# Graph network in two passes: degrees and relation counts turned in 32x32 blocks on VectorE and spread by DRAM reloads, instead of by TensorE

## The chip, the cores and the metric

The kernel runs on one core of one Trainium2 chip. The metric is the device time of one execution in microseconds (us), as the median over runs. The profile is of one execution on the same core, recorded by the hardware profiler.

## What is computed

The input `x` is (128 graphs, 64 nodes, 768 features), `adj` a 0/1 matrix (128, 64, 64), the same for both layers. In layer 0 `adj` also serves as the relation index, and the reference is written for general relation numbers.

```
# layer 0
h   = relu(layernorm(x))
deg = adj.sum(-1);  rdeg = adj^T.sum(-1);  deg_c, rdeg_c = (the same, 1 where 0)
ctx = adj   @ (h @ Wadj.T + badj) / deg_c
    + adj^T @ (h @ Wrev.T + brev) / rdeg_c
    + h @ Wself.T + bself
rel = einsum(adj,   E[rels]) @ Wr.T  + br  * deg
    + einsum(adj^T, E[rr])   @ Wrr.T + brr * rdeg      # rr: reversed relations, NUM_BASE higher
x   = x + ctx + rel
# layer 1
h    = relu(layernorm(x))
hw   = h @ W (6 heads of 128);  logits from tanh(hw), w_src, w_dst;  leaky relu; masked by adj
out  = softmax(logits) @ hw + b;  elu;  gate = sigmoid(h @ H_w.T + H_b)
x    = x + gate * out + (1 - gate) * h
```

## The kernel before

**Tiling.** A tile is 128 rows of 768 features, two graphs (GT = 2, N = 64). Two tiles make a pair; there are NT = 64 tiles and NP = 32 pairs. Pass 1 does layer 0 for pair after pair, pass 2 layer 1. In pass 1 the three operands of a pair (graph average with `adj`, with its transpose, and the rows themselves) meet the three weights. The products over 3x3 blocks of the weights are done as 15 products with sums of blocks (a fast matrix product, `PRODUCTS`, with the operand sums `f1` to `f11` formed on VectorE by `form`, L351 and L353). Pair 0 uses plain products (`PLAIN`).

**Steps and their order.** `main(p)` gives a list of about 91 steps, one per (product, k block, operand): each step is one f32 128x128 by 128x256 matmul (L754), which the profile shows as two records. After the last step of a product that is read out, `add` (L746, L748) adds or subtracts its PSUM bank (`pwa`, `pwb`, or one half of `pwcd`) into `X`. `beside(p)` lists the other work: what finishes pair p - 1 and what prepares pair p + 1. The table `BESIDE` gives the step of `main` ahead of which each piece is issued. `merged` weaves the two lists. All engines and the DMA queue of SyncE (SP) are in program order, so `BESIDE` fixes the order on each queue. Pairs 2 to 31 are in `SHARED`: for them the own rows come as turned blocks by `turn_own`, `put_own` (L551) and `load_own` (L565) through DRAM.

**Degrees.** `degrees` (step "deg") multiplies a block matrix of ones (`blkb`) with the bf16 adjacency on TensorE (L607), so that every row of a graph holds the column sums; VectorE clamps them out of PSUM (L609). `one_over` (step "over") takes the reciprocal over 256 columns (L613), and `over_degrees` (step "rts") multiplies the adjacency by it (L618) into `rts`, which the operand matmuls (`operands`, L682, step "ops") use as moving data; ScalarE copies their results out of PSUM (L692).

**Counts.** `prep_c`, `ids_worth` and `ids_sum` count on VectorE how often each relation number occurs in a row of the adjacency (packed as digits), and `digits` (step "dig") unpacks them to `cnt`, 81 values per row (78 counts, two flags, one 1). GpSimd (POOL) writes each value three times in a row into `c3` (L653). `count_t` (steps "ct0" and "ct1") transposes `c3` on TensorE in two parts per tile, 126 and 117 columns (L661), and ScalarE copies them out to `cntT` (L664). `counts` (L738) multiplies `cntT` with the table `tabs`, in which each of the 81 rows stands as three bf16 parts, and accumulates into the bank of the product that is read next. So `cntT` of pair p + 1 is made ahead of step 90 of pair p and first read after product a01 of pair p + 1 (steps 12 to 17).

PSUM: `pwa` and `pwb` have one bank each, `pwcd` two; the buffer `pb` (two of them) is shared by the degree product, the count transposes and the operand matmuls.

## Time and profile before

| | |
|---|---|
| median of 3 runs | 2358.45 us (2357.53 to 2358.49) |
| profiled execution | 2358.5 us, span 2356.7 us |
| mean granted TensorE clock | 0.994 |
| pass 1 ends (last `pwcd` count matmul) | 1425.4 us |
| degree products L607 on TensorE | 32, mean duration 273 ns |
| count transposes L661 on TensorE | 128, median duration 219 ns |
| copies of the counts L664 on ScalarE | 128, median 269 ns |
| reciprocal L613 on VectorE | 32, mean 1744 ns |
| copies L653 on POOL | 64, mean 436 ns |

In the page's rows a group is given as line, engine, operation, out<-in, shapes, count, then busy us and mean ns, then the idle time of the engine ahead of it with what ended it. PE is TensorE's matmul stream and PEld its weight loads, DVE is VectorE, ACT ScalarE. A timeline row gives the start, the length, and the operation with a count of merged instructions. Matmuls are pipelined: a record's duration overlaps with the next one's.

### The profile page before, as it was taken

Reading aid. Unit: us, or ns where it says so; the run is one execution under the profiler, and the core shown is the slowest. Engines: PE = TensorE matmul, PEld = TensorE weight load, DVE = VectorE, ACT = ScalarE, POOL = GpSimd, SP = SyncE. Lnnn points to the kernel's source line nnn. Section 1 sums busy time; section 2 is a strip of 40 time slices with the busy share of each in tenths; the row PEclk is TensorE's granted clock in tenths of the full one; section 3 lists DMA queues with packets and bytes.
Section 4 is the critical chain, followed back from the end, with each engine's and each line's share of the span. In section 5 each row is a group of like instructions: output and inputs, shape, how many; then the busy total and the mean of one; then the engine's idle time right before and its main releaser. Section 6 shows DMA issues by size and latency. Waiting matters only on the chain.

```text
span 2356.7 us, 35546 instructions
## 1 busy us (share of the span) xinstructions
PE 2326.5 (99%) x11591; PEld 1654.2 (70%) x11591; DVE 1979.0 (84%) x3673; ACT 1304.5 (55%) x3955; POOL 434.1 (18%) x983
## 2 busy tenths in 40 slices
PE   9999999999999999999999999999999999999996
PEld 7888888888888888888888885444444444444444
DVE  8878778777787787787787777899999999999997
ACT  3454454454554554554554533677766776777775
POOL 1111111111111111111111111122222222222222
PEclk9999999999999999999999999999999999999997
DMA  6334435335335335335334357577777776676776
GB/s 188 83 90 125 119 90 136 106 90 143 100 93 147 93 97 152 90 96 147 90 103 139 90 162 145 117 146 142 152 144 150 141 148 140 138 145 138 148 136 132
DMA packets 706907, 296.19 MB, mean 126 GB/s; under 512 B 524586, under 2 KB 657053, under 8 KB 706722
## 3 DMA queue, kind: packets, MB, share of 16 engines
q1 hardware_dynamic: 696850, 269.11, 46.5%
q0 software_dynamic: 9728, 24.78, 6.0%
q8 instruction: 91, 1.49, 0.3%
q14 instruction: 94, 0.77, 0.1%
q10 hardware_dynamic: 144, 0.04, 0.0%
HBM read 131.85 MB, written 136.45 MB: 114 GB/s over the span
## 4 chain that ended last, share of the span: by engine, by line
PE 94%; DVE 2%; DMA 2%; issue 1%; ACT 0%; SPq 0%; POOL 0%; POOLq 0%; DVEq 0%; ACTq 0%
PE pwa L754 21%; PE pwb L754 17%; PE pwcd L754 14%; PE pma L1059 13%; PE pmb L1059 11%; PE pmd L1059 5%; PE pmc L1059 4%; PE pb L682 3%; PE ps L1224 1%; PE pwcd L738 1%; PE pwcd L682 1%; DVE weights L353 1%; PE ps L1163 1%; DMA weights<-in_wrev_t_dram 1%; PE pmc L1224 0%
## 5 line engine op out<-in xcount | busy, mean ns | idle before, releaser
L754 PE MATMUL pwa<-weights,op 128*128 128x256 f32 x2304 | 539.4, 381 | 0.3 <-DVE x L746 0.3
L754 PEld LDWEIGHTS pwa<-weights,op 128*128 128x128 f32 x2304 | 422.3, 190 | 53.8 <-issue 1.1
L754 PE MATMUL pwb<-weights,op 128*128 128x256 f32 x1932 | 454.5, 381 | 0.0
L754 PEld LDWEIGHTS pwb<-weights,op 128*128 128x128 f32 x1932 | 359.4, 190 | 53.1 <-issue 0.2
L353 DVE TENSOR_TENSOR op<-op 128x768 f32<-128x768 f32 x310 | 291.5, 949 | 95.6 <-ACT op L692 91.7
L754 PE MATMUL pwcd<-weights,op 128*128 128x256 f32 x1560 | 357.8, 379 | 0.0
L754 PEld LDWEIGHTS pwcd<-weights,op 128*128 128x128 f32 x1560 | 296.1, 190 | 40.1
L1059 PE MATMUL pma<-weights,op_f 128*128 128x512 f32 x620 | 291.2, 592 | 0.0
L1111 ACT ACTIVATE pr<-pr 128x128 f32<-128x128 f32 x768 | 225.6, 295 | 92.3 <-DVE pr L1101 90.5
L692 ACT COPY op<-pb 128x512 f32<-128x512 f32 (+1 forms) x132 | 70.8, 618 | 320.5 <-PE pb L682 320.5
L1059 PEld LDWEIGHTS pma<-weights,op_f 128*128 128x128 f32 x620 | 117.7, 190 | 147.4 <-issue 139.0
L330 POOL TENSOR_SCALAR rn<-su 128x1 f32<-128x1 f32 x124 | 28.1, 227 | 901.9 <-ACT hf L325 531.0
L1059 PE MATMUL pmb<-weights,op_f 128*128 128x512 f32 x372 | 180.9, 594 | 0.0
L540 ACT ACTIVATE hp<-x,rn 128x768 f32<-128x768 f32 x60 | 107.8, 1797 | 109.7 <-POOL rn L332 109.7
L1111 ACT ACTIVATION_READ_ACCUMULATOR pr<-pr 128x1 f32 x768 | 143.6, 187 | 0.0
L324 ACT ACTIVATE hf<-x 128x768 f32<-128x768 f32 x64 | 53.6, 837 | 150.1 <-DVE x L790 150.1
L1184 ACT ACTIVATE pb<-al,mx 128x64 f32<-128x64 f32 x384 | 128.1, 336 | 12.3 <-DVE mx L1176 12.2
L1059 PEld LDWEIGHTS pmb<-weights,op_f 128*128 128x128 f32 x372 | 68.4, 190 | 84.0 <-issue 75.8
L1285 POOL DMA_DIRECT2D out_dram<-f x62 | 55.0, 887 | 390.0 <-DVE f L1282 382.6
L746 DVE TENSOR_TENSOR x<-pwa,x 128x256 f32<-128x256 f32 x96 | 40.4, 421 | 99.8 <-PE pwa L738 72.0
L1059 PE MATMUL pmb<-weights,h 128*128 128x512 f32 x248 | 122.5, 596 | 0.0
L1059 PE MATMUL pmc<-weights,op_f 128*128 128x512 f32 x248 | 121.8, 592 | 0.0
(232 smaller groups left out, 4219.3 us busy)
## 6 DMA issues: line engine op xcount, KB each, us to landing
x<-in_x_dram SPq DMA_DIRECT2D x64, 384.0 KB
h<-ht SPq DMA_DIRECT2D x64, 384.0 KB
out_dram<-x SPq DMA_DIRECT2D x64, 384.0 KB
hh<-hh SPq DMA_DIRECT2D x64, 384.0 KB
h<-h SPq DMA_DIRECT2D x256, 96.0 KB
x<-hh SPq DMA_DIRECT2D x64, 384.0 KB
out_dram<-f POOLq DMA_DIRECT2D x62, 384.0 KB, 6.5
h<-hpt SPq DMA_DIRECT2D x60, 384.0 KB
```

What stands on the lines that cost most here:

```text
L324: nc.scalar.activation(by, src, AF.Copy, scale=-1.0 / D, accum_out=sums[:, 0:1])
L330: nc.gpsimd.tensor_scalar(to[:, 0:1], sums[:, 1:2], 1.0 / D, EPS, op0=OP.mult, op1=OP.add)
L353: return (nc.vector.tensor_add if s1 == "+" else nc.vector.tensor_sub)(to, x, y)
L540: nc.scalar.activation(hp.rearrange("p (b f i) -> p b f i", b=KB, f=NQ), X[t].rearrange("p (b i f) -> p b f i", b=KB, f=NQ), AF.Relu, scal ...
L682: nc.tensor.matmul(to[:, g, :, i, :], H0[2 * p + k][o, kb * P : (kb + 1) * P], rts[p % 2][o, k, :n].rearrange("p s n -> p (s n)"), start=T ...
L692: nc.scalar.copy(a[:, :n].rearrange("p s h (g n) -> p g (s h) n", g=GT), ps[:, :, c * n * KQ * N : (c + 1) * n * KQ * N].rearrange("p g (x ...
L746: nc.vector.tensor_add(v, bank[b][:, :CQ], v)
L754: nc.tensor.matmul(bank[b][:, :CQ], OPS[p, an][:, s, q, :], bw[bn][:, (s * KQ + q) * CQ : (s * KQ + q + 1) * CQ], start=(first and q == s ...
L1059: nc.tensor.matmul(bank[p, b], operand(p, an)[:, q, :], bw2[bn][:, 2 * q * CQ : 2 * (q + 1) * CQ], start=(first and q == 0), stop=(q == KQ ...
L1111: nc.scalar.activation(PR[t][:, j, h, :], PR[t][:, j, h, :], AF.Copy, accum_out=to)
L1184: nc.scalar.activation(PB[t][:, h, :], AL[t][:, h, :], AF.Exp, bias=MX[t][:, h : h + 1], accum_out=DN[t][:, h : h + 1])
L1285: nc.gpsimd.dma_start(of[t * P : (t + 1) * P, :], FF[t], accum_op=OP.add)
```

## The change

For pairs 2 to 31 the degree product on TensorE is replaced. VectorE reduces the adjacency along the row, for it and its transpose (`row_degrees`; the numbers of the column sums are the row sums of the other one), clamps and inverts the 4 columns, and turns a 128x32 tile in 32x32 blocks; the turned block goes to DRAM (`put_degrees`) and comes back with each graph's degrees spread over its 64 partitions (`get_degrees`). `over_row_degrees` then multiplies as before.

The counts of these pairs are placed by POOL in six copies into one standing tile `c3s` of 2 tiles x 2 parts x 128 columns, turned by one VectorE instruction of 512 columns (`turn_counts`), stored to DRAM (`put_counts`), and read back so that the blocks come to their places (`get_counts`). The table is laid out anew: two parts of 128 rows each, the unused rows zero. Pairs 0 and 1 keep the degree product and the transposes on TensorE, with `c3s` written by ScalarE and one copy out of PSUM per tile. The diff, with lines left out of the table `BESIDE`:

```diff
--- before.py
+++ after.py
@@ -83,14 +83,7 @@
 IN_PLACE = {"f3": "a12", "f2": "a10"}
-BESIDE = {... "f2": 20, "f3": 21, "dev1": 22, "deg": 26, "prepc": 26, ... "over": 36, ... "rts": 48, ...
-          "dig": 67, "a01": 68, "load": 68, "eturn1": 79, "etput1": 82, "ops": 83, "f1": 83, "f7": 83,
-          "ct0": 88, "ct1": 89}
+BESIDE = {... 'f2': 20, 'deg': 20, 'f3': 21, 'dev1': 22, 'putd': 24, 'prepc': 26, ... 'getd': 34, ...
+          'rts': 50, ... 'dig': 67, 'a01': 68, 'load': 68, 'ct': 75, 'putct': 78, 'eturn1': 79,
+          'etput1': 82, 'ops': 83, 'f1': 83, 'f7': 83, 'getct': 87}
 PLACES = ("g6", "g10", "b11", "b21", "g12", "w", "g14", "b01", "b10", "b20", "b02", "b12", "b22",
@@ -225,10 +218,9 @@
     NROW = NCNT + 3
-    PARTS = ((0, P // 3), (P // 3, NROW))
     assert NV == 3 * NG and DIGIT ** 3 <= 1 << 24
     assert GT == 2 and N == 64 and DO == P and H == KB and KB % 6 == 0 and H % 2 == 0
-    assert 3 * (NROW - P // 3) <= P and NT % 2 == 0 and HALF <= 512
+    assert 2 * 32 <= NROW and 3 * NROW <= 2 * P and NT % 2 == 0 and HALF <= 512
     xf = x.rearrange("g n d -> (g n) d")
     of = out.rearrange("g n d -> (g n) d")
@@ -244,6 +236,8 @@
     H0D = [dram.tile([KB * P, P], F32, name=f"h0_{t}") for t in range(NT)]
+    CTD = [dram.tile([4 * P, P], BF16, name=f"ct_{p}") for p in range(NP)]
+    RDD = [dram.tile([Q, P], F32, name=f"rd_{p}") for p in range(NP)]
     PTD = [dram.tile([KB // 2 * P, P], F32, name=f"pt_{t}") for t in range(NT)]
     H1D = [[dram.tile([KB * P, P], F32, name=f"h1_{p}_{k}") for k in range(2)] for p in range(NP)]
@@ -461,7 +455,18 @@
         nc.vector.tensor_copy(identb, ident)
-        tabs = [wa.tile([3 * (b - a), D], BF16, name=f"tab{a}") for a, b in PARTS]
+        tabs = wa.tile([P, 2, D], BF16, name="tabs")
+        R2 = NROW - 2 * Q
+        PLACED = ((0, 0, 0, 0, Q), (1, 1, 0, 0, Q), (2, 2, 0, 0, Q), (0, 3, 0, Q, Q), (1, 4, 0, Q, Q),
+                  (2, 5, 0, Q, Q), (0, 6, 0, 2 * Q, R2), (1, 7, 0, 2 * Q, R2),
+                  (2, 6, R2, 2 * Q, Q - R2), (2, 7, R2, 3 * Q - R2, 2 * R2 - Q))
+        nc.vector.memset(tabs[:, 1], 0.0)
+        c3s = wa.tile([P, 2, 2, P], BF16, name="c3")
+        nc.vector.memset(c3s, 0.0)
+        dgs = wa.tile([P, Q], F32, name="dgs")
+        nc.vector.memset(dgs, 0.0)
@@ -521,8 +526,10 @@
             nc.scalar.copy(q[:NROW], v[:NROW])
             if i < 2:
                 nc.vector.tensor_sub(v[:NROW], v[:NROW], q[:NROW])
-            for (a, b), tab in zip(PARTS, tabs):
-                nc.sync.dma_start(tab[i : 3 * (b - a) : 3, :], q[a:b, :])
+            for c, f, at, v0, n in PLACED:
+                if c == i:
+                    a = NQ * at + f % NQ
+                    nc.sync.dma_start(tabs[a : a + NQ * (n - 1) + 1 : NQ, f // NQ, :], q[v0 : v0 + n, :])
         H0, ADF, AB, CNT, CT_T, GR, WO, SUM, HF, HH_, HT = ({} for _ in range(11))
         OPS = {}
@@ -578,13 +585,47 @@
                 nc.vector.tensor_copy(af, AI[p])
                 nc.vector.tensor_copy(ab, af)
+        DGR, RD = {}, {}
+        def row_degrees(p):
+            dg = DGR[p] = small.tile([P, 2, 2], F32, name="dg")
+            nc.vector.tensor_reduce(dg, ADF[p], AX.X, OP.add)
+        def turn_degrees(p):
+            row_degrees(p)
+            d = dgs
+            v = d[:, :4].rearrange("p (k d) -> p k d", k=2)
+            nc.vector.tensor_scalar(v, DGR[p], 1.0, None, op0=OP.max)
+            nc.vector.reciprocal(v, v)
+            RD[p] = small.tile([P, Q], F32, name="dt", bufs=1)
+            nc.vector.transpose(RD[p], d)
+        def put_degrees(p):
+            nc.sync.dma_start(RDD[p].rearrange("c (b n) -> b c n", n=Q), RD[p])
+        def get_degrees(p):
+            rd = RD[p] = work.tile([P, 4, N], F32, name="rd", bufs=1)
+            for g in range(GT):
+                at = RDD[p][0:4, g * N : (g + 1) * N]
+                nc.sync.dma_start(rd[g * N : (g + 1) * N],
+                                  bass.AP(tensor=at.tensor, offset=at.offset,
+                                          ap=[[0, N], *at.ap]))
+        def over_row_degrees(p):
+            rd = RD[p].rearrange("p (k d) n -> p k d n", k=2)
+            for d in range(2):
+                nc.vector.tensor_mul(rts[p % 2][:, :, d, :], ADF[p][:, :, 1 - d, :], rd[:, :, d, :])
         def prep_c(p):
             af, ab = ADF[p], AB[p]
-            cnt = CNT[p] = work.tile([P, 2, NROW], BF16, name="cnt")
-            dg = small.tile([P, 2, 2], F32, name="dg")
-            nc.vector.tensor_reduce(dg, af, AX.X, OP.add)
+            cnt = CNT[p] = work.tile([P, 2, NROW], BF16, name="cnt", bufs=1)
+            if p not in SHARED:
+                row_degrees(p)
+            dg = DGR[p]
             nc.vector.tensor_scalar(cnt[:, :, NCNT : NCNT + 2], dg, 1.0, None, op0=OP.min)
             nc.vector.memset(cnt[:, :, NCNT + 2 : NCNT + 3], 1.0)
             gr = GR[p] = work.tile([P, 2, 2, N], BF16, name="gr")
@@ -648,20 +689,39 @@
             nc.vector.tensor_copy(
                 CNT[p][:, :, :NCNT].rearrange("p k (d v) -> p k d v", d=2),
                 di.rearrange("p (k d) i v -> p k d (i v)", k=2))
+            for f, n, at, v0, w in ((0, 3, 0, 0, Q), (3, 1, 0, Q, Q), (4, 2, 0, Q, Q), (6, 2, 0, 2 * Q, R2),
+                                    (6, 1, R2, 2 * Q, Q - R2), (7, 1, R2, 3 * Q - R2, 2 * R2 - Q)):
+                c3 = c3s.rearrange("p k i (f n) -> p k i f n" if p in SHARED else
+                                   "p k i (n f) -> p k i f n", f=NQ)
+                put = nc.gpsimd.tensor_copy if p in SHARED else nc.scalar.copy
+                put(c3[:, :, f // NQ, f % NQ : f % NQ + n, at : at + w],
+                    CNT[p][:, :, None, v0 : v0 + w].to_broadcast([P, 2, n, w]))
+        def turn_counts(p):
+            ct = CT_T[p] = work.tile([P, 4, P], BF16, name="ct", tag="eq", bufs=1)
+            nc.vector.transpose(ct.rearrange("p a n -> p (a n)"),
+                                c3s.rearrange("p k i n -> p (k i n)"))
+        def put_counts(p):
+            nc.sync.dma_start(CTD[p].rearrange("(q p) n -> p q n", p=P), CT_T[p])
+        def get_counts(p):
+            ct = work.tile([P, 2, 2, P], BF16, name="cntT", bufs=2)
+            nc.sync.dma_start(
+                ct.rearrange("p k i n -> p (k i n)").rearrange("p (b n) -> p b n", n=Q),
+                CTD[p].rearrange("(b i) (f n) -> (i f) b n", i=Q, n=Q))
             for k in range(2):
-                c3 = CT_T[p, k] = work.tile([P, NROW, 3], BF16, name="c3")
-                nc.gpsimd.tensor_copy(c3, CNT[p][:, k, :, None].to_broadcast([P, NROW, 3]))
+                CT_T[p, k] = ct[:, k]
         def count_t(p, k):
-            c3 = CT_T[p, k]
             pn = pss.tile([P, 2, 512], F32, name="pb")[:, 0, :P].bitcast(BF16).rearrange(
                 "p (i n) -> p i n", i=2)
-            cn = CT_T[p, k] = work.tile([P, 2, P], BF16, name="cntT", bufs=4)
-            for i, (a, b) in enumerate(PARTS):
-                nc.tensor.transpose(pn[: 3 * (b - a), i, :],
-                                    c3[:, a:b, :].rearrange("p v c -> p (v c)"), identb)
-            for i, (a, b) in enumerate(PARTS):
-                nc.scalar.copy(cn[: 3 * (b - a), i, :], pn[: 3 * (b - a), i, :])
+            if k == 0:
+                CT_T[p] = work.tile([P, 2, 2, P], BF16, name="cntT", bufs=2)
+            cn = CT_T[p, k] = CT_T[p][:, k]
+            for i in range(2):
+                nc.tensor.transpose(pn[:, i, :], c3s[:, k, i, :], identb)
+            nc.scalar.copy(cn, pn)
         def operands(p, *calls, last=False):
@@ -734,9 +794,9 @@
                 k, q = int(c[0]), int(c[1])
                 if first:
                     new(b)
-                for i, (a, e) in enumerate(PARTS):
-                    nc.tensor.matmul(bank[b][:, :CQ], CT_T[p, k][: 3 * (e - a), i, :],
-                                     tabs[i][:, q * CQ : (q + 1) * CQ],
+                for i in range(2):
+                    nc.tensor.matmul(bank[b][:, :CQ], CT_T[p, k][:, i, :],
+                                     tabs[:, i, q * CQ : (q + 1) * CQ],
                                      start=(first and i == 0), stop=True, skip_group_check=True)
             def add(b, c, sign="+"):
@@ -953,9 +1013,10 @@
                 steps.update({
                     "prep": lambda: prep(n),
                     "dev0": lambda: dev(n, 0), "dev1": lambda: dev(n, 1),
-                    "deg": lambda: deg(n),
+                    "deg": lambda: turn_degrees(n), "putd": lambda: put_degrees(n),
+                    "getd": lambda: get_degrees(n),
                     "norm0": lambda: norm(n, 0), "norm1": lambda: norm(n, 1),
-                    "over": lambda: one_over(DEG[n]), "rts": lambda: over_degrees(n, DEG[n]),
+                    "rts": lambda: over_row_degrees(n),
                     "turn0": lambda: turn_own(2 * n), "put0": lambda: put_own(2 * n),
                     "turn1": lambda: turn_own(2 * n + 1), "put1": lambda: put_own(2 * n + 1),
                     **{a: lambda a=a: load_own(n, a) for a in ("a10", "a01", "a11", "a00", "a12", "a02")},
@@ -966,7 +1027,8 @@
                     "dig": lambda: digits(n),
                     "f1": lambda: form(n, "f1"), "f7": lambda: form(n, "f7"),
                     "load": lambda: load(n + 1),
-                    "ct0": lambda: count_t(n, 0), "ct1": lambda: count_t(n, 1)})
+                    "ct": lambda: turn_counts(n), "putct": lambda: put_counts(n),
+                    "getct": lambda: get_counts(n)})
             return sorted([(BESIDE[k], f) for k, f in sorted(steps.items(), key=lambda e: place_of[e[0]])]
                           + more, key=lambda e: e[0])
```

## The prediction

> **What bounds the kernel now.** I read the page first (busy shares, the slices, the chain that ended last), then the timeline of TensorE over one pair in the steady part of pass 1, then the groups of instructions that the change touches, then the DMA view.
>
> ```profile
> PE 2326.5 (99%) x11591; PEld 1654.2 (70%) x11591; DVE 1979.0 (84%) x3673; ACT 1304.5 (55%) x3955; POOL 434.1 (18%) x983
> ...
> PEclk9999999999999999999999999999999999999997
> ...
> PE 94%; DVE 2%; DMA 2%; issue 1%; ACT 0%; SPq 0%; POOL 0%; POOLq 0%; DVEq 0%; ACTq 0%
> ```
>
> TensorE is busy 99% of the span at full clock, and 94% of the chain is TensorE. "Busy" overlaps here (a matmul's duration includes the tail that the next one hides), so a price must come from start times. This is the TensorE timeline where one pair ends and the next begins (start us, us, ...):
>
> ```profile
> 763.45 2.32 PE L754 MATMUL pwb<-weights,op 128*128 128x256 f32 x10
> 765.70 2.06 PE L682 MATMUL pb<-r,h 64*128 64x128 f32 x32
> 767.59 1.06 PE L682 MATMUL pwcd<-r,h 64*128 64x128 f32 x16
> 768.58 0.70 PE L754 MATMUL pwb<-weights,op 128*128 128x256 f32 x2
> 769.12 0.39 PE L738 MATMUL pwb<-tab,cntT 126*128 126x256 bf16 x2
> 769.34 1.89 PE L754 MATMUL pwa<-weights,op 128*128 128x256 f32 x8
> 771.07 0.27 PE L661 MATMUL pb<-identb,c 128*126 128x128 bf16 x2
> 771.18 0.65 PE L754 MATMUL pwa<-weights,op 128*128 128x256 f32 x2
> 771.67 0.28 PE L661 MATMUL pb<-identb,c 128*126 128x128 bf16 x2
> 771.78 0.65 PE L754 MATMUL pwa<-weights,op 128*128 128x256 f32 x2
> 772.26 0.39 PE L738 MATMUL pwa<-tab,cntT 126*128 126x256 bf16 x2
> ...
> 784.16 0.27 PE L607 MATMUL pb<-ab,blkb 128*128 128x256 bf16 x1
> 784.27 1.89 PE L754 MATMUL pwb<-weights,op 128*128 128x256 f32 x8
> ```
>
> The reader is to see that no row carries an idle entry: in the waits of TensorE nothing at all stands between 75 and 1380 us. The same operand row starts at 721.98 one pair earlier, so a pair takes 43.72 us. It is made of 180 f32 records at 0.2158 (12 start in 2.59 us) = 38.85, 48 operand records 2.88, 12 count records at 0.1125 = 1.35, and the transposes and degree product, 0.44 (below). That leaves 0.20, nearly all around the operand block (ten records there take 2.25 instead of 2.16, two take 0.54 instead of 0.43). So in pass 1 the time is the number of TensorE instructions; taking some out shortens each pair, unless something is then late.
>
> **The change, part by part** (pairs 2 to 31 take the new road: 30 pairs).
>
> *Degree product removed.* From 784.16 to the next start at 784.27: 0.11 us a pair.
>
> *Four count transposes removed.* From 771.07 to 772.26 is 1.19 us, and the four f32 records inside account for 0.86: 0.33 a pair. By slot the four cost 4 x 0.057 = 0.23; the other 0.10 is two 51 ns semaphore instructions at this line (60 in all), with which their weight loads waited for POOL's copy. The group's mean is 219 ns, and the Trainium skill (TensorE: Matmul & The Clock Gate, Part 4: PE-mode transpose) likewise gives about 275 ns for a bf16 transpose in a kernel. Charged like that the five instructions would be 4 x 0.275 + 0.273 = 1.37 a pair, 41 us in all. The starts say 0.44, because the next matmul begins inside the duration; I take the starts. **30 x 0.44 = 13.2 us.**
>
> *The count matmuls* now use 128 rows, where they used 126 and 117. Both old forms have the same slot (0.1125), so 0.
>
> *ScalarE.* Four copies of 0.27 us are gone (L664), 1.1 us a pair. It is 55% busy and its next work merely starts sooner: 0.
>
> *VectorE, degrees.* Removed: the clamp from PSUM (0.425) and this reciprocal:
>
> ```profile
> L613 DVE RECIPROCAL rd<-rd 128x256 f32<-128x256 f32 x32 | 55.8, 1744 | 0.0
> ```
>
> In their place come a clamp and a reciprocal over 4 columns (rows of that size: 0.18 each) and a 32-column transpose. The transposes of 384 and 768 columns take 0.567 and 0.953, so 0.18 plus 1.0 ns a column: 0.21. The reduction (0.41) is the old one, moved from step 26 to step 20, in front of f3, which so ends about 1.0 us later: some 740.4 instead of 739.46, where its product starts at 742.28. Cover 1.9 us. The add behind it (739.78) slips to about 740.8; its bank is wanted again at 744.87. Afterwards VectorE is about 1.6 us ahead, in the stretch (743 to 758 us) where it is full. No TensorE wait is there to be cured: 0.
>
> *VectorE, counts.* One transpose of 512 bf16 columns: 0.70 if it goes like f32, 0.44 if two-byte columns went twice as fast; no bf16 transpose is in the trace, the f32 rows are near, I take 0.70. In sum VectorE loses 2.17 and gains 1.27 a pair.
>
> *POOL and VectorE's new wait.* Two copies of 243 elements (0.39 each) become six with the same elements in all. Each lies between 0.19 (the smallest POOL operation) and 0.39, together 1.1 to 2.4 us; I take 1.6. POOL has nothing else there (it sat idle 8.3 us before these copies). The transpose (step 75) follows them and waits: digits end at 761.6, POOL at about 763.2, the transpose at about 763.9. Queued behind it on VectorE are the subtraction of pwa (763.65 now), eturn1's transpose (763.99), and f1 and f7, which start at 768.01 when ScalarE is through. VectorE idles 1.74 before the subtraction and 3.06 before f1 today, so f1 is not touched; pwa is wanted at 769.34. Cost 0; without that cover each us late at f7 would show on TensorE beyond the 2.3 us between f7's end (770.0) and 772.71.
>
> *Degrees through DRAM.* One store of 128 rows, two loads of 512 rows together. The store is issued at about 739 behind put0's 384 KB, which is through by 739; the link then stands idle until 749.5. SP sits in getd until the store has landed. Behind getd on SP is put1, which is not ready before 749.3. From issue to release a put took 3.3 us (put1 issued at 749.3, load_own released at 752.60); twice that is 745.6, and the reader (step 50) starts near 752.7. Cover 7 us: 0.
>
> *Counts through DRAM.* The store has 512 rows of 256 B, the reload 2048 rows of 64 B. The own-operand loads give the price: a full microsecond (756.5 to 757.5) of their 128 B rows is
>
> ```profile
> DMA packets 1543, 0.20 MB, mean 195 GB/s; under 512 B 1543, under 2 KB 1543, under 8 KB 1543
> ```
>
> so 2048 rows are 1.3 us if a 64 B row costs what a 128 B row does (0.7 if only bytes counted). The store is issued near 764 behind pair loads that keep the link busy to 767.5, and lands by 768; SP waits in getct until then, with only the next pair's put0 (780.16) behind it. The reload lands by 772 and is first read by the weight load before 780.48. Cover 8 us: 0. POOL issues none of these; SP issues five DMAs more a pair at about 0.45 us, 2.3 us of a queue that mostly waits.
>
> A rule speaks against this: the Trainium skill (VectorE: DVE Perf Modes, The three transpose paths) says that a transpose by access pattern is 19 times slower than the DMA's own transpose, given as 1309 ns for 128x128. As an estimate from that page, four tiles would be 4 x 25 = 99 us a pair, and the kernel about twice as slow. Here the element-wise turning stays on VectorE and the DMA moves runs of 32 elements, so I price it by the 1543 packets; no run shows a 64 B run yet.
>
> *Start, and pairs 0 and 1.* The three new memsets are about 0.8 us on VectorE (128x64 words took 0.11), against 0.72 idle before the adjacency lands: 0.1. Ten table DMAs instead of six, at 0.77 each on SP, end at about 37.8 and land near 40; first use at 42.16: 0. Six ScalarE copies twice, 1.4 us each by L664: 30.95 to 38.37 is nearly free, the second delays operand copies at 58.5 by under 1 us, read at 63.28. Bounds 0 to 1 us; I take 0.2.
>
> **Sum.** The profiled execution took 2358.5 (span 2356.7 and 1.8 around it), the median is 2358.45, so nothing need be shifted. 2358.5 - 13.2 + 0.2 = **2345.5**.
>
> **Rivals.**
>
> *Part is given back on TensorE.* The count weight loads now wait for a DMA, the transposes waited for POOL with 51 ns a time. Two to four such instructions a pair return 3 to 6 us, a little stall at f3 as much: about 2350. For: the gaps around the operand block. Against: today's count weight loads wait for ScalarE almost without such instructions (2 in all).
>
> *Nothing is won.* The removed slots turn into a wait for something that already ended just in time: 2358. Against: f7, the tightest, has 2.3 us and loses only 0.33.
>
> *The reload is late (slower).* It is one wait on TensorE before a01's counts. It decides when the reload takes more than about 10 us from its start (8 times the row's price). At 12 us, 2 us over, TensorE waits 30 x 2 = 60 us: 2405. For: the trap above, and SP's wait for the store. Against: the packet row.
>
> **How the numbers follow.** Full saving 0.76 (own range 2341 to 2350), part given back 0.10, nothing won 0.06, reload late 0.08. What a measurement of this kernel can tell is 0.2%, 4.7 us: faster 0.86, same 0.06, slower 0.08. The low end 2340 adds the 0.10 us beside two operand-adjacent records going too (30 x 0.10 = 3) and a free start; the high end 2353 takes in a saving cut to 5.
>
> **What would show it.** Right: no L607 or L661 record in pairs 2 to 31; operand blocks 43.28 us apart; TensorE's waits still empty in pass 1; last pwcd record near 1412 instead of 1425.4; reciprocal near 0.18 us; the 512-column transpose 0.4 to 0.7. Wrong: a wait of the count matmuls on a DMA, of pwa's or f3's product on VectorE, VectorE's transpose waiting for POOL over 5 us, or a pair period of 43.7 or more.

## The result, and the profile after

The changed kernel takes 2344.31 us (median of 4 runs, 2343.59 to 2344.68), the kernel before 2357.99 beside it (4 runs, 2355.35 to 2358.49). The ratio is 0.9944, 95% interval 0.9927 to 0.9961. The profiled execution took 2344.68 us, its span 2342.8, at a mean clock of 0.996. The prediction was 2345.5 (2340 to 2353). The total agrees, but three of its terms were off and nearly cancel, so the terms are what is to be looked at.

From the page of the changed kernel, the busy shares, the granted clock and the chain that ended last:

```profile
PE 2310.5 (99%) x11441; PEld 1645.8 (70%) x11441; DVE 1953.3 (83%) x3736; ACT 1280.8 (55%) x3843; POOL 439.6 (19%) x1099
...
PEclk9999999999999999999999999999999999999998
...
PE 95%; DMA 2%; DVE 1%; issue 1%; ACT 1%; SPq 0%; POOL 0%; POOLq 0%; DVEq 0%; ACTq 0%
```

TensorE is still the bound, with 150 records fewer: 120 transposes and 30 degree products. The same stretch of the TensorE timeline that the prediction showed (start us, us, operation) now reads:

```profile
758.62 2.32 PE L814 MATMUL pwb<-weights,op 128*128 128x256 f32 x10
760.87 2.06 PE L742 MATMUL pb<-r,h 64*128 64x128 f32 x32
762.76 1.06 PE L742 MATMUL pwcd<-r,h 64*128 64x128 f32 x16
763.75 0.70 PE L814 MATMUL pwb<-weights,op 128*128 128x256 f32 x2
764.28 0.38 PE L798 MATMUL pwb<-tabs,cntT 128*128 128x256 bf16 x2
764.50 2.75 PE L814 MATMUL pwa<-weights,op 128*128 128x256 f32 x12
767.09 0.38 PE L798 MATMUL pwa<-tabs,cntT 128*128 128x256 bf16 x2
```

The twelve f32 records that were cut into 8, 2 and 2 by the transposes now run in one piece, from 764.50 to 767.09. The operand block comes at 760.87 here and at 804.12 in the next pair, 43.25 us apart (43.249 over all pairs of the steady part; 43.722 before). In the waits of TensorE from 75 to 1380 us (engine, line, what it waited for, us, times, longest) there are two, both the first adds behind pair 0:

```profile
PE pwa L814 <- DVE x L806: 0.3, 1, 0.3
PE pwcd L798 <- DVE x L806: 0.3, 1, 0.3
```

Where the time went, by starts in the two traces:

| part | before | after | difference |
|---|---|---|---|
| 30 pairs in the steady part, each | 43.722 | 43.249 | -0.473, x30 = -14.2 |
| last count matmuls of pair 0 (`pwcd`) start | 72.94 | 75.34 | +2.4 |
| last count matmuls of pass 1 (`pwcd`) start | 1425.36 | 1413.53 | -11.8 |
| pass 2, from there to the end of the span | 931.3 | 929.3 | -2.1 |
| span | 2356.7 | 2342.8 | -13.9 |

The last row but one is not shown to be the change's. Counted from pass 2's first matmul, the same records start at the same time in both traces, to 0.05 us, until some 40 us before the end; the difference arises behind that. From that matmul to the end of the span, the executions profiled here range from 926.1 to 932.4 us, without regard to what was done in pass 1. In a repeat of the changed kernel (below), pass 1 ends at 1413.37 and pass 2 takes 1.5 us more than here; the medians there, 2357.59 and 2345.89, are 11.7 us apart, which is what pass 1 gives.

The work beside TensorE, in the timelines of POOL and VectorE (a bracket is idle time ahead, and what ended it):

```profile
756.76 1.22 POOL L697 COPY c<-cnt 128x192 bf16<-128x192 bf16 x6 [10.22 <-DVE cnt L689]
...
758.01 0.71 DVE L702 STREAM_TRANSPOSE ct<-c 128x512 bf16<-128x512 bf16 x1 [0.98 <-POOL c L697]
```

VectorE waits 0.98 us a pair for POOL's six copies; the new wait is real, and TensorE does not wait for VectorE there.

### The profile page after: what moved, and what is told of

Its sections match the earlier page's. It is cut to its first block, busy times and chain, and to the rows that moved or that the text cites. A ratio compares the mean times of both kernels' runs of the same rounds, so it can differ in the third digit from the quotient of the medians.

```text
span 2342.8 us, 35503 instructions
## 1 busy us (share of the span) xinstructions
PE 2310.5 (99%) x11441; PEld 1645.8 (70%) x11441; DVE 1953.3 (83%) x3736; ACT 1280.8 (55%) x3843; POOL 439.6 (19%) x1099
## 4 chain that ended last, share of the span: by engine, by line
PE 95%; DMA 2%; DVE 1%; issue 1%; ACT 1%; SPq 0%; POOL 0%; POOLq 0%; DVEq 0%; ACTq 0%
PE pwa L814 21%; PE pwb L814 18%; PE pwcd L814 14%; PE pma L1121 14%; PE pmb L1121 11%; PE pmd L1121 5%; PE pmc L1121 5%; PE pb L742 3%; PE ps L1286 1%; PE pwcd L798 1%; PE pwcd L742 1%; PE ps L1225 1%; PE pmc L1286 0%; DVE weights L347 0%; DMA weights<-in_wself_t_dram 0%
## 5 line engine op out<-in xcount | busy, mean ns | idle before, releaser
L814 PE MATMUL pwa<-weights,op 128*128 128x256 f32 x2304 | 529.6, 379 | 0.3 <-DVE x L806 0.3
L814 PEld LDWEIGHTS pwa<-weights,op 128*128 128x128 f32 x2304 | 427.5, 190 | 56.0 <-issue 1.1
L752 ACT COPY op<-pb 128x512 f32<-128x512 f32 (+1 forms) x132 | 70.8, 618 | 355.2 <-PE pb L742 355.2
L806 DVE TENSOR_TENSOR x<-pwcd,x 128x256 f32<-128x256 f32 x127 | 53.4, 420 | 81.6 <-PE pwcd L798 81.5
```

Of the source, the lines that this page charges most:

```text
L752: nc.scalar.copy(a[:, :n].rearrange("p s h (g n) -> p g (s h) n", g=GT), ps[:, :, c * n * KQ * N : (c + 1) * n * KQ * N].rearrange("p g (x ...
L806: nc.vector.tensor_add(v, bank[b][:, :CQ], v)
L814: nc.tensor.matmul(bank[b][:, :CQ], OPS[p, an][:, s, q, :], bw[bn][:, (s * KQ + q) * CQ : (s * KQ + q + 1) * CQ], start=(first and q == s ...
```

## The experiments

Each kernel is the changed one with one edit. The medians of the kernel before, in the three groups of runs, were 2357.68, 2357.23 and 2357.59. Since pass 2's end varies by some microseconds, the spacing of the operand blocks is what is compared first. The totals agree with it: against the repeat's 2345.89, the first three kernels below take 3.3, 9.8 and 20.1 us more, and 30 times their spacing gives 3.3, 10.1 and 20.1.

### The two halves, each undone by itself

**The degrees back on TensorE.**

```diff
-'f3': 21, ... 'deg': 20, 'putd': 24, 'getd': 34, 'rts': 50
+'f3': 21, ... 'deg': 26, 'over': 36, 'rts': 48
-"deg": lambda: turn_degrees(n), "putd": ..., "getd": ..., "rts": lambda: over_row_degrees(n)
+"deg": lambda: deg(n), "over": lambda: one_over(DEG[n]), "rts": lambda: over_degrees(n, DEG[n])
...
-if p not in SHARED:                    # in prep_c
-    row_degrees(p)
+row_degrees(p)
```

> The changed kernel with its degree part alone undone: for pairs 2 to 31 the degree product, the clamp out of PSUM and the reciprocal over 256 columns are back, the store and the two loads of the degrees are gone; the counts stay on the new road. Theory (slots of TensorE decide): the operand blocks move apart by the product's slot, 43.25 to 43.36 us, so 30 x 0.11 = 3.3 us, 2347.6. Rival (the instruction costs its duration, 0.273 us): 43.52, 8.2 us, 2352.5. Rival (VectorE's relief was what counted): 2.2 us more of VectorE work a pair shows as waits of TensorE, over 2355.

Measured: 2349.21 (2348.18 to 2350.3), ratio 0.9963 (0.995 to 0.9976). The pair takes 43.360, +0.111. That is the slot read from starts (0.11), not the 273 ns duration. The reciprocal over 256 columns (1749 ns here) is back on VectorE and costs TensorE nothing, and no wait of TensorE for it appears, so what VectorE lost or gained by this half is indeed free.

**The count transposes back on TensorE.**

```diff
-'ct': 75, 'putct': 78, 'getct': 87
+'ct0': 88, 'ct1': 89
-"ct": lambda: turn_counts(n), "putct": ..., "getct": ...
+"ct0": lambda: count_t(n, 0), "ct1": lambda: count_t(n, 1)
...
-c3 = c3s.rearrange("p k i (f n) -> p k i f n" if p in SHARED else "p k i (n f) -> p k i f n", f=NQ)
+c3 = c3s.rearrange("p k i (n f) -> p k i f n", f=NQ)
```

> The changed kernel with its count part alone undone: for pairs 2 to 31 the four transposes on TensorE and one copy per tile on ScalarE are back (on 128 columns each, with the new table of 128 rows), VectorE's transpose of 512 columns, the store and the reload are gone; the degrees stay on the new road. Theory: four slots of 0.057 and two semaphore instructions of 0.05, 43.25 to 43.58 us a pair, 30 x 0.33 = 9.9 us, 2354.2. If the semaphore instructions do not come back, 43.48 and 2351.2. Rival (duration 0.219 each): 0.88 a pair, 26 us, 2370. The TensorE waits in pass 1 stay empty in all three.

Measured: 2355.69 (2353.66 to 2356.68), ratio 0.999 (0.9982 to 0.9999). The pair takes 43.583, +0.335. The two halves add up: 0.111 + 0.335 = 0.446 of the 0.473 that the change saves.

**Eight transposes more.** To see what one transpose among f32 matmuls costs, and where, four pairs of transposes of a constant were added to each pair of tiles, away from every wait.

```diff
+def two_more():
+    pn = pss.tile([P, 2, 512], F32, name="pb")[:, 0, :P].bitcast(BF16).rearrange("p (i n) -> p i n", i=2)
+    for i in range(2):
+        nc.tensor.transpose(pn[:, i, :], blkb, identb)
+more += [(i, lambda: two_more()) for i in (24, 30, 36, 42) if n in SHARED]
```

> The changed kernel with eight more bf16 128x128 transposes a pair on TensorE (pairs 2 to 31), of a constant, two each ahead of steps 24, 30, 36 and 42, into PSUM that nobody reads: no wait is added, so this is the price of the instruction alone. Theory (slot of 0.057): 0.46 a pair, period 43.71, 13.7 us, 2358.0. Rival (duration 0.219 each): 1.75 a pair, 45.0, 2396.9. Rival (the page's 275 ns each): 2.2 a pair, 45.45, 2410.3.

Measured: 2366.02 (2364.75 to 2367.47), ratio 1.0036 (1.0022 to 1.0049). The pair takes 43.918, +0.669, or 0.167 for two transposes. The duration (219 ns in the trace, 275 ns by the Trainium skill, TensorE: Matmul & The Clock Gate, Part 4) would have made it 1.75 to 2.2 us, and is refuted as a price; but so is the bare slot of 0.057. The TensorE timeline of this kernel shows both parts:

```profile
741.91 2.76 PE L820 MATMUL pwa<-weights,op 128*128 128x256 f32 x12
744.50 0.28 PE L730 MATMUL pb<-identb,blkb 128*128 128x128 bf16 x2
744.61 2.81 PE L820 MATMUL pwb<-weights,op 128*128 128x256 f32 x12
747.26 0.28 PE L730 MATMUL pb<-identb,blkb 128*128 128x128 bf16 x2
```

The two transposes hold the stream for 744.61 - 744.50 = 0.11. The twelve f32 records behind them start 747.26 - 744.61 = 2.65 before the next thing, where twelve behind a count matmul take 744.50 - 741.91 = 2.59. So some 0.055 us more is borne by the f32 records that follow. Taken record by record in this trace, it is the first of them alone: 0.272 us to the next start, where 0.216 is usual. Behind two count records, and behind the degree product in the kernel before, which are bf16 too, the first f32 record takes 0.218, so the change of type alone is not the reason; what is stays open. These transposes wait for nothing and have no semaphore instruction, and they cost what the removed ones did.

**126 and 117 rows again in the count matmuls.** The table's rows beyond those are left out.

```diff
+r = (126, 117)[i]
-nc.tensor.matmul(..., CT_T[p, k][:, i, :], tabs[:, i, ...], ...)
+nc.tensor.matmul(..., CT_T[p, k][:r, i, :], tabs[:r, i, ...], ...)
```

> The changed kernel with the count matmuls over 126 and 117 rows of the turned counts and of the table again, instead of 128 twice; the table's other rows are left out of the sum. It asks where the 0.03 us a pair comes from by which the pairs became shorter than the removed instructions account for (43.72 to 43.25 measured, 0.44 forecast). Theory (a count matmul over all 128 rows starts its successor a little sooner, 0.219 against 0.226 for two): the period goes back up by 0.03 to 0.05, 1 to 1.5 us in all. Rival (it is elsewhere, in the operand block or the semaphore instructions): period 43.25 unchanged, 2344.3.

Measured: 2348.23 (2345.84 to 2348.72), ratio 0.9958 (0.9942 to 0.9975). The pair takes 43.275, +0.026, which is the piece that the two halves left over: 0.446 + 0.026 = 0.472. By starts, two count records take 0.218 us with all 128 rows and 0.225 without; that is 0.039 for the twelve of a pair, and the f32 records among them take back 0.012. The 0.026 are 0.8 us over 30 pairs; the rest of the total's 3.9 us is not from pass 1, as pass 2 took 931.2 us in its profiled execution.

### How much cover the reload has

**The reload of the counts three and six times over.**

```diff
-nc.sync.dma_start(
+for _ in range(3):          # 6 in the other kernel
+  nc.sync.dma_start(
```

> The changed kernel with the reload of the turned counts done three times in a row into the same tile, each waiting for the one before to land (pairs 2 to 31). It probes the cover of the reload. In the changed kernel the reload is issued at 761.5 and its packets end near 764; the first reader's matmul starts at 775.3. Theory (some 10 us of cover): with about 3 us from issue to landing the third lands near 771, nothing waits, the period stays 43.25 and the time 2344. Rival (the reload lands just in time): two more of 3 us put 6 us a pair on TensorE, 180 us, 2524.

> The same with the reload done six times in a row. Theory: at about 3.2 us each the sixth lands near 781, 5 to 6 us after the reader wants it (775.1), and what was hidden shows as a wait of the count matmul on the DMA: period 48 to 50 us, 30 x 5.5 = 165 us more, about 2510 (2450 to 2560). If each takes 2.3 us or less, the sixth is in time too and the time is 2344.

Measured with three: 2345.59, a single run. The pair stays at 43.25 except for one, in which SP issues three other small loads (`dl`, from 199.77) shortly ahead of the reloads (204.05) and TensorE waited 2.2 us:

```profile
PE pwcd L799 <- DMA cntT<-ct: 2.2, 1, 2.2
```

Three times the transfer fits in all other pairs, so the cover is real: in the changed kernel the reload is issued at 761.49 and first read at 775.30. TensorE at this one wait:

```profile
214.86 0.39 PE L799 MATMUL pwcd<-tabs,cntT 128*128 128x256 bf16 x2 [2.21 <-DMA cntT<-ct]
215.09 2.76 PE L815 MATMUL pwa<-weights,op 128*128 128x256 f32 x12
217.68 2.75 PE L815 MATMUL pwb<-weights,op 128*128 128x256 f32 x12
```

The twelve f32 records behind it take 2.59 us from start to start, as always, so this wait cost no more than its own length.

Measured with six: 2577.34, a single run. The waits of TensorE:

```profile
PE pwcd L799 <- DMA cntT<-ct: 158.8, 30, 10.8
```

That is 5.3 us a pair, but the span is 232.8 us longer. The TensorE timeline of this kernel shows what else there is:

```profile
750.26 0.61 PE L799 MATMUL pwcd<-tabs,cntT 128*128 128x256 bf16 x2 [5.09 <-DMA cntT<-ct]
750.67 4.87 PE L815 MATMUL pwa<-weights,op 128*128 128x256 f32 x12
755.37 2.75 PE L815 MATMUL pwb<-weights,op 128*128 128x256 f32 x12
```

The twelve f32 records behind the wait take 4.70 us from start to start instead of 2.59. By stretches (us, busy time of each engine, granted clock, DMA share, GB/s):

```profile
749.00:751.00 2.00, 0.73 (x3) 0.68 (x4) 0.09 (x1) 1.97 (x3) 0.00 (x0) 0.50 1.07 236
751.00:754.00 3.00, 3.00 (x8) 2.36 (x8) 2.90 (x7) 0.19 (x1) 0.00 (x0) 0.50 0.03 5
754.00:756.00 2.00, 2.00 (x8) 1.63 (x7) 0.46 (x4) 0.00 (x0) 0.00 (x0) 0.77 0.05 8
756.00:760.00 4.00, 4.00 (x20) 3.52 (x19) 3.83 (x11) 0.00 (x0) 0.00 (x0) 1.00 0.14 33
```

After 5 us without work TensorE has half its clock until about 755, 5 us more. The 30 waits are 4.0 to 10.8 us long, and the twelve records behind them take 3.85 to 5.12 us; together that is 65 of the 74 us that the waits leave over. The Trainium skill (TensorE: Matmul & The Clock Gate, Part 1) has this rule: the clock is halved after an idle window of about 3.4 us and comes back after as long a busy one. The run agrees in the factor; the recovery here is somewhat longer, from 750.3 to about 755. So 5.3 us of waiting cost 232.8 / 30 = 7.8 us a pair. The prediction's rival of a late reload charged a wait with its length alone; for the 2 us that it named, the wait of 2.2 us above bears that out, and for waits of this length it is too low.

**The counts turned element by element in the reload.** The block transpose on VectorE is dropped, and four loads of 16,384 runs of two bytes do the whole turning.

```diff
-'ct': 75, 'putct': 78
+'putct': 78
-c3 = c3s.rearrange("p k i (f n) -> p k i f n" if p in SHARED else "p k i (n f) -> p k i f n", f=NQ)
+c3 = c3s.rearrange("p k i (n f) -> p k i f n", f=NQ)
...
-nc.sync.dma_start(CTD[p].rearrange("(q p) n -> p q n", p=P), CT_T[p])
+nc.sync.dma_start(CTD[p].rearrange("(p q) n -> p q n", q=4), c3s.rearrange("p k i n -> p (k i) n"))
...
-ct.rearrange("p k i n -> p (k i n)").rearrange("p (b n) -> p b n", n=Q), CTD[p].rearrange("(b i) (f n) -> (i f) b n", ...)
+for q in range(4):
+    nc.sync.dma_start(ct[:, q // 2, q % 2, :], CTD[p].rearrange("(n q) c -> q c n", q=4)[q])
```

> The changed kernel without VectorE's transpose of the counts: POOL's tile is stored to DRAM as it is, and four loads of 128 rows by 128 elements read it back element by element in turned order, 65536 runs of 2 bytes a pair instead of 2048 of 64. It asks what the 32x32 turning on VectorE is worth, and tests the rule of the Trainium skill on transposes by access pattern (VectorE: DVE Perf Modes, The three transpose paths). Estimate from the packet row (1543 packets in a microsecond): 42 us of link time a pair next to 17 that are there, about 60 us a pair instead of 43.25, 2850 us. Estimate from the page (19 times 1309 ns for each of four tiles, 99 us, beside the 17): about 116 us a pair, 4500 us. Rival (hidden): under 30 us and 2344.

Measured: 3563.5, a single run; pairs of 75 to 103 us, 84 in the mean. Both estimates missed, one below and one above. SyncE's queue (start us, us, DMA issues):

```profile
950.20 54.51 SPq L710 DMA_DIRECT2D cntT<-ct  x3
1004.81 18.20 SPq L558 DMA_DIRECT2D h<-hpt  x1
```

One load keeps the issuing queue for 18 us (54.51 over 3; the median of all is 14.0), and the next thing behind it is held up as well. In one microsecond of it (986 to 987) the DMA view has

```profile
DMA packets 847, 0.00 MB, mean 2 GB/s; under 512 B 847, under 2 KB 847, under 8 KB 847
```

against 1543 packets for the 128-byte rows of before, at a DMA share of 0.45 only. So the DMA engines are not full, while the issuing queue is held; the limit seems to lie with the issue of such runs, though no run here shows this by itself. The trap of the Trainium skill that the prediction weighed (VectorE: DVE Perf Modes, The three transpose paths) comes out here in its order of size, 14 to 18 us a load against the 25 estimated from the page for a 128x128 tile. The page states it for a large innermost stride at the destination, a condition that the prediction left out; in this kernel the stride is at the source. The change does not fall into it, because VectorE turns the blocks and the reload moves 64-byte runs. These go about as fast per run as the 128-byte ones, at a DMA share of 0.92 (half a microsecond of the changed kernel, 763.0 to 763.5):

```profile
DMA packets 733, 0.05 MB, mean 94 GB/s; under 512 B 733, under 2 KB 733, under 8 KB 733
```

### The 2.4 us lost in pair 0

From the first f32 matmul to 76 us, three waits of TensorE stand in the changed kernel, of which the one for `x` was there before (0.5):

```profile
PE pb L742 <- ACT op L752: 1.7, 1, 1.7
PE pwcd L798 <- DVE x L806: 0.3, 1, 0.3
PE pb L648 <- ACT ab L583: 0.3, 1, 0.3
```

The first stops the operand matmuls that stood at 57.54 before. They want a buffer `pb` that ScalarE has to empty. In the kernel before, TensorE and then ScalarE went:

```profile
57.54 1.57 PE L682 MATMUL pb<-r,h 64*128 64x192 f32 x16
```

```profile
49.67 1.50 ACT L692 COPY op<-pb 128x768 f32<-128x768 f32 x2 [4.51 <-PE pb L682]
58.50 1.50 ACT L692 COPY op<-pb 128x768 f32<-128x768 f32 x2 [7.33 <-PE pb L682]
```

In the changed kernel:

```profile
60.15 1.62 PE L742 MATMUL pb<-r,h 64*128 64x192 f32 x16 [1.72 <-ACT op L752]
```

```profile
58.16 1.29 ACT L697 COPY c<-cnt 128x192 bf16<-128x192 bf16 x6 [12.18 <-DVE cnt L689]
59.31 1.49 ACT L752 COPY op<-pb 128x768 f32<-128x768 f32 x2
```

The operand copies (L752) are ready to go when the operand matmuls that started at 49.53 are through, at about 51. They stand behind the six copies of the counts of pair 1, which wait for VectorE's counts until 58.16: ScalarE has been idle for 12.18 us. In the trace of before the same operand copies ran at 49.67 and 58.50, without such a neighbour. The wait for `ab` is the same on a smaller scale, the adjacency of pair 1 copied behind pair 0's six copies. Counted from the first f32 matmul (14.62 before, 15.09 after), pair 0 takes 58.32 before and 60.25 after: 1.93 us are from these two waits, less 0.2 by which the wait for `x` is shorter. The other 0.47 lies ahead of that first matmul, and is not a fixed cost of the change: in the seven kernels above, which do the same up to there, it starts between 14.50 and 14.67 (at 14.50 in four of them).

**These copies on POOL, for pairs 0 and 1 too.**

```diff
-put = nc.gpsimd.tensor_copy if p in SHARED else nc.scalar.copy
+put = nc.gpsimd.tensor_copy
```

> The changed kernel with the six copies into the count tile on POOL for pairs 0 and 1 too, instead of on ScalarE. In the changed kernel pair 0 ends 2.40 us later than in the kernel before. Theory: 0.4 of it is the degree product of pair 1 waiting for the adjacency copy that stands on ScalarE behind the six copies, and 1.8 the operand matmuls at 60 us waiting for a PSUM copy behind the other six; both go, the wait of 1.72 us at 60 us is gone from TensorE's waits, and the count matmul at 75.3 us starts 1.8 to 2.2 us sooner: 2342.3. Rival (the first pair is late from its start on, from the memsets or a slower clock there): it stays at 75.3, and the time at 2344.3. The last 30 us of the kernel differ by some 2 us between executions of one kernel, so the early times in the trace decide, not the total.

Measured: 2349.89 (2345.43 to 2351.49), ratio 0.9962 (0.9949 to 0.9976); pair 0 ends at 78.11, later than with the change itself. The waits for ScalarE are gone, but the forecast gain fell: POOL is no free place there. POOL, and VectorE in the same stretch:

```profile
58.07 6.53 POOL L697 COPY c<-cnt 128x192 bf16<-128x192 bf16 x6 [21.14 <-DVE cnt L689]
```

```profile
57.82 1.75 DVE L345 SCALAR_TENSOR_TENSOR weights<-weights 128x1536 f32<-128x1536 f32 x1
59.49 1.91 DVE L347 TENSOR_TENSOR weights<-weights 128x1536 f32<-128x1536 f32 x1
61.43 1.76 DVE L345 SCALAR_TENSOR_TENSOR weights<-weights 128x1536 f32<-128x1536 f32 x1
```

Six copies of 0.2 to 0.34 us in the steady part take 6.53, single ones up to 2.07, as long as one of VectorE's instructions beside it. The kernel before had this in the same place without harm: POOL's two copies for pair 1 took 3.61 us there, 0.39 each in the steady part. The Trainium skill (SBUF — State Buffer, Who interferes with whom) says that a VectorE instruction with two inputs in SBUF contends with a GpSimd one that reads SBUF, over ports that one of the two holds alone; all three are of that kind, and the numbers fit. TensorE then waits for the copies:

```profile
PE pb L723 <- POOL c L697: 3.2, 2, 2.8
```

Behind these waits the clock is lost too: the next twelve f32 records take 4.33 us from start to start (64.72 to 69.05, granted clock 0.54 to 0.66), and 2.65 in the changed kernel (63.64 to 66.29, clock 1.00).

**The changed kernel once more, and the copies moved to later steps.** The six copies become a step of their own, behind the operand copies in ScalarE's order. The first kernel is the changed one without an edit, for comparison on the same chip.

> The changed kernel itself once more, beside the next two on the same chip, and to see how its last 60 us vary. Theory: pass 1 repeats to 0.5 us (last count matmul near 1413.5, operand blocks 43.25 apart), and pass 2, 928.26 then, comes out anywhere between 926.8 and 932.4 as in the runs so far, since the granted clock of the last 30 us changes (0.66 to 0.77). Rival: pass 2 repeats as well, and its 2.1 us less than before belong to the change.

```diff
+            if p in SHARED:
+                place(p)
+        def place(p):
             for f, n, at, v0, w in (...):          # the six copies
...
+            (27, lambda: place(0)),
-            (84, lambda: count_t(1, 0)),
+            (81, lambda: place(1)),
+            (88, lambda: count_t(1, 0)),
```

> The changed kernel with ScalarE's six copies of pairs 0 and 1 issued later: pair 0's behind the last table part (27), pair 1's behind the operand copies of step 80 (81), and the first transposes of pair 1 at 88 instead of 84. Theory: the loss of pair 0 came from the order on ScalarE, where these copies wait for VectorE's counts and the copy of the adjacency and of the operand sums stood behind them. The wait of 1.72 us at 60 us goes, the last count matmul of pair 0 starts near 73.4 instead of 75.34, and about 2 us come off: 1411.6 for the last count matmul, 2342.3 in all. Rival (PSUM is only waited for elsewhere, at pair 1's transposes): 75.3 stays.

Measured: the changed kernel again 2345.89 (2343.89 to 2347.35), ratio 0.9946 (0.9933 to 0.996), pair 0 ending at 75.19 with a wait of 1.7 us in the same place. Pass 1 repeats to 0.2 us (1413.37) and pass 2 does not (929.7 us instead of 928.3 from its first matmul), so the theory held against the rival. With the later copies 2343.01 (2340.28 to 2344.77), ratio 0.9934 (0.9921 to 0.9946), pair 0 ending at 72.60. TensorE and ScalarE of this kernel:

```profile
57.36 1.57 PE L747 MATMUL pb<-r,h 64*128 64x192 f32 x16
```

```profile
58.33 1.50 ACT L757 COPY op<-pb 128x768 f32<-128x768 f32 x2 [7.33 <-PE pb L747]
59.71 1.32 ACT L702 COPY c<-cnt 128x192 bf16<-128x192 bf16 x6
```

The operand copies are first now, and both waits on ScalarE are gone. The median of this kernel is below those of both given ones. From the first f32 matmul (at 14.94 and 14.50) to there it takes 58.10 instead of 60.25 (the same 60.25 in the first execution and in the repeat), 2.15 us less, and no longer than before the change (58.32). That the median is 2.9 lower is in line with it, though the two intervals overlap.

**The three memsets moved behind the first matmuls**, to step 10 of the first pair, on top of the edit above.

```diff
-        nc.vector.memset(tabs[:, 1], 0.0)
-        nc.vector.memset(c3s, 0.0)
-        nc.vector.memset(dgs, 0.0)
+        def zeros():
+            for v in (tabs[:, 1], c3s, dgs):
+                nc.vector.memset(v, 0.0)
...
+            (10, lambda: zeros()),
```

> The same as the one before, with the three new memsets on VectorE moved from the start to step 10. In the changed kernel the first f32 matmuls come 0.47 us later than before, at 15.09 instead of 14.62; the eight operand records at 9.9 us take 1.51 instead of 0.92 us, while the granted clock reads 1.00 in both. Theory (the memsets delay the start): 14.6 again, pair 0 ends near 72.9, 2341.8. Rival (a slow phase of TensorE's clock that falls on other instructions by chance): 15.0 stays, and the sum is that of the kernel before it, 2342.3.

Measured: 2343.26 (2339.64 to 2344.92), ratio 0.9934 (0.9922 to 0.9947). Nothing was won: the first f32 matmul starts at 14.41, and at 14.50 with the memsets in their old place. So they do not make up the 0.47. What makes the start vary between 14.4 and 15.1, with the same work ahead of it, stays open.

## Why the prediction held, and where it did not

*The bound and the way of pricing.* Right. TensorE's stream sets the time of pass 1, and prices read from start to start carried over: 0.111 for the degree product and 0.335 for the four transposes when each was undone, against 0.11 and 0.33. Prices by duration were refuted by the degree product (0.273) and by the eight transposes more.

*The 0.10 us ascribed to two semaphore instructions.* Right in size, wrong in cause. Transposes that wait for nothing cost 0.167 for two as well, and with the transposes put back, 30 such instructions stand in the trace instead of 60, at the same price. The extra is borne by the first f32 record behind each two transposes. The semaphore instructions only stood beside it.

*The count matmuls, put at 0.* Mis-sized: with all 128 rows they are 0.026 us a pair shorter, 0.8 us in all. With that, and with prices of 0.446 where 0.44 was taken, the saving is 14.2 rather than 13.2.

*"Start, and pairs 0 and 1 ... I take 0.2", with bounds 0 to 1.* The largest miss: 2.4 us by this trace, beyond its own bounds. The step that failed is "the second delays operand copies at 58.5 by under 1 us, read at 63.28". It asked when the copies at 58.5 are read and overlooked the other side of the same buffers. The operand copies before them, ready at about 51, were queued behind the six as well, and the next operand matmuls, at 57.5, need the bank that those copies set free. The sum also called the first six copies "nearly free", and the adjacency copy behind them held up the degree product of pair 1 by some 0.4 us. The later order of the copies removed that wait and the smaller one and won 2.15 us, which settles this cause for the 1.93 us; the other 0.47 is a variation of the start that stays unexplained.

*The covers.* Right, each with room: VectorE waits 0.98 us for POOL and TensorE never for VectorE there; the six copies took 1.22 (1.6 assumed); the transpose of 512 bf16 columns 0.71 (0.70), the reciprocal 0.178; no wait of TensorE stands at the products of f3, f1 or f7. The 64-byte runs of the reload go nearly at the packet price (733 in half a microsecond against 1543 in one), and three reloads in a row still fit in all pairs but one.

*The rival in which part is given back.* It did not happen: the pairs are 43.249 us apart, below the 43.28 forecast, and the count weight loads have four semaphore instructions in the whole changed kernel, all before 42 us, and two before.

*The chance of 0.08 for a late reload.* The mechanism exists (six times the reload shows it), but three times the reload was still hidden but for one pair. Its price of a wait by length alone agrees with the one wait of 2.2 us and is too low for waits of 4 us and more, as the clock was left out.

*The sum.* -14.2 + 2.4 is -11.8 at the end of pass 1, where the prediction had -13.0. That only 1.2 us remain is in part luck: the saving was 1.0 larger than forecast, and pairs 0 and 1 cost 2.2 more. By pass 1 alone the total would be 2346.7; pass 2's tail, 2.1 us shorter in this execution, took it from 1.2 above the forecast to 0.8 below, and the repeat, at 2345.89, lies between the two.

## What to carry to other kernels

When a matmul stream is full, price a removed instruction from start to start and include how the instructions behind it go; then undo each part alone and see whether the pieces add up to the whole, as they did here to 0.001 us a pair. A copy moved to another engine's queue must be asked two questions: who reads what stands behind it, and who needs the buffers that this frees. A wait that a change can cause on TensorE should be charged with the clock that may be lost afterwards: waits of 1.7 and 2.2 us cost only themselves here, two of 0.4 and 2.8 us close together 1.7 us more, and 5.3 us of wait were 7.8.

## What the runs showed of the hardware that was not expected

- Two bf16 transposes in an f32 stream cost about 0.055 us beyond their own slots of 0.11, all of it on the first f32 record behind them; two count matmuls or the degree product do not.
- Count matmuls over 128 rows take less time than over 126 and 117: 0.218 against 0.225 us for two.
- Loads of two-byte runs hold the issuing queue for 14 us (median) and move 847 packets in a microsecond at a DMA share of 0.45, where 64-byte runs go at 733 in half a microsecond.
- POOL's copies took up to 2.07 us instead of 0.34 beside VectorE instructions with two inputs of 1536 columns.
- After 5 us of waiting, TensorE's granted clock was 0.50 for about 5 us; after waits of 1.7 and 2.2 us it was 1.00.
